# Layer 0 of a four-layer graph network: where the 1/norm broadcast, the rank prefix sums and the rank loads stand in the order of work

## The chip, the cores and the metric

The kernel runs on one NeuronCore of a Trainium2 chip. It is one launch, and all four layers are in it. The metric is the time of an execution on the device in microseconds (us). Three runs of the kernel before took 1393.85, 1397.64 and 1398.86 us; the median is 1397.64 us. The profile is of a further execution, which took 1403.91 us, with a span of 1402.0 us from the first instruction to the last.

## The reference, cut to what matters

N = 2708 nodes, D = 512 features, `adj` is a sparse N x N matrix of float32 values with a nonzero diagonal, denser in its first rows and columns. Only layer 0 is touched by the change:

```python
h = maximum(layernorm(x), 0)                     # (N, D)
head = (adj > 0).astype(float32)
head = head / maximum(sqrt(sum(head * head, axis=-1, keepdims=True)), 1e-12)
inc = adj + head                                 # = adj + mask * 1/norm of the row
x = x + (inc @ h) / sum(inc, axis=-1, keepdims=True)
```

`head * head` summed over a row is the number of nonzeros of the row, so a row needs one number for its head, `rn` = 1/sqrt(count), and one for its degree. Layer 1 (attention, which for these scores comes down to the largest entry of each row of `adj`), layer 2 (two products with `adj`, two dense layers) and layer 3 (a product with the mask of `adj`) follow.

## The kernel before, in words

The rows are cut in 22 tiles of 128 (the last has 20). In layer 0 the loop at L780 to L838 takes one row tile m after the other. Its product `inc @ h` is not done over all 2708 columns: the first six column tiles (DENSE = 6) are taken whole, and of the rest only the columns in which one of the tile's rows has a nonzero. These are found on the chip, per row tile, and are brought in by indirect DMAs on POOL in chunks of 128 columns (CHUNKS, L39: 8 chunks for tile 3, 7 for tiles 4 to 7, 6 for 8 to 14, 5 or 6 for 15 to 20, 2 for 21). Row tiles 0 to 2 (LEAD) are taken over all columns.

For a row tile k >= 3 the steps are these, and they are spread over several passes of the loop:

- Row statistics, `row_norm` and `row_sum` (L523, L543): the slab `ar` of 128 full rows (1354 KB) is loaded, ACT takes the signs (L534), their count (L538), rn (L539) and the row sum (L549). `attended` (L555) takes the largest entry of each row and its place on DVE (L561, L562). Slabs have three buffers.
- `count` (L292): for each group of three row tiles PE adds the signs up over the rows (L302), which gives for each column the number of nonzeros that each row tile has in it.
- `rank_blocks` (L343): DVE makes 0 or 1 of the counts and sums them over each quarter of the columns (L351). PE turns the sums into the offset of each quarter (`ahead`, L355), ACT copies it (L356), DVE scans (L357) and adds the end mark (L358), and SP writes the result, the rank of each column, to DRAM in four pieces (`rank_b`, L361). For the last row tile and for tiles 1 and 2, `rank_rows` (L366) does the same in one row each, from the counts in DRAM (L375, L376, L379), and is put on the list `todo` as a job of its own.
- `load_ranks` (L387): SP reads the ranks of one row tile back, the same row to all 128 partitions (485 KB; two buffers).
- `search` (L400): DVE looks up the place of the 1st, 2nd, 3rd ... nonzero column in the ranks (L407, L409, L413) and writes the indices idx_g and idx_a (L414, L422).
- `gather_adj` (L566): POOL gathers the columns of `adj` (tile `ac`, three buffers, 64 KB each chunk). `gather_rows` (L586): POOL gathers the rows of h into the slots of `h` (16 slots, 256 KB each chunk).
- `incidence` (L624): PE spreads the rn of the 128 rows along the free axis (`rb`, L629, a PSUM tile with one buffer). DVE makes inc = adj + mask * rb for the dense columns (tile `inc`) and for the listed ones (tile `incl`), in two instructions each (L634, L642). The listed `ac` is written to DRAM for the later layers (L657, `lst`).
- Products (L792): first six dense ones, then the listed ones, into one PSUM bank. Every product is a matmul of float32, which the profile shows as two PE instructions.
- `after` (L725): the projection of tile m - 2 (L158, four products) and the transposes of tile m - 1 (L192). Then DVE scales and adds (L805) and normalizes for layer 1 (L176 to L186).

The jobs on `todo` are done by `do_next` (L677): one for each row tile whose statistics are made, and, once all are made, one for each pass of the loop, two in passes 15 and 16. Before a search runs, its ranks are loaded, and after each call the ranks of the next search are. `stats_to` (L688) holds the statistics up to eight row tiles ahead of the products. `gathers_to` (L716) gathers the columns of tile m + 3 and the rows of tile m + 2 at the end of pass m, where the search is done by then. `flush` (L755) issues the stores that were put off.

The order on each engine's queue is set by a scheduler at build time, which keeps the order of the program where costs and due times don't tell otherwise. `tc.issue_after(ins)` puts what is traced in its block behind `ins` on that instruction's engine. [...]

In pass m the incidence of tile m + 1 is traced ahead of the products of tile m (L787, L788).

Of the kernel before, what the change touches and what calls it, by code (L numbers as in the profile page):

```python
# [9 lines left out]
FP = mybir.dt.float32  # L10
# [12 lines left out]
P = 128  # L23
# [13 lines left out]
DENSE = 6  # L37
LEAD = 3
# [4 lines left out]
def kernel(  # L43
# [31 lines left out]
    NT = (N + P - 1) // P  # L75
# [52 lines left out]
    WIDE, LOW = (N - BEHIND) // 4, BEHIND // 2  # L128
# [97 lines left out]
    with tc.tile_pool(name="l0_slab", bufs=2) as slabs, tc.tile_pool(  # L226
        name="l0_h", bufs=1
    ) as hp, tc.tile_pool(name="l0_w", bufs=2) as wp, tc.tile_pool(
        name="l0_acc", bufs=2, space=PSUM
    ) as ps_acc, tc.tile_pool(name="l0_small", bufs=1, space=PSUM) as ps_small, tc.tile_pool(  # L230
        name="l0_list", bufs=3, space=PSUM
    ) as ps_list, tc.tile_pool(name="l0_tr", bufs=1, space=PSUM) as ps_tr, tc.tile_pool(
        name="l0_y", bufs=1, space=PSUM
# [109 lines left out]
        def rank_blocks(ms, last_block):  # L343

            wide = WIDE
            row_end = hp.tile([P, WIDE + 1], HF, name="rk")
            rk, end = row_end[:, :wide], row_end[:, wide : wide + 1]
            sums, offs = (wp.tile([P, 1], FP, name=name) for name in ("sums", "offs"))  # L350
            nc.vector.tensor_scalar(  # L351
                rk, last_block, 1.0, None, op0=ALU.min, op1=ALU.add, accum_out=sums
            )
            ahead = ps_list.tile([P, BLK], FP, name="list")
            nc.tensor.matmul(ahead[:, :1], ahead_of, sums, start=True, stop=True)  # L355
            nc.scalar.copy(offs, ahead[:, :1])  # L356
            nc.vector.tensor_tensor_scan(rk, rk, rk, offs[:, 0:1], ALU.add, ALU.max)  # L357
            nc.vector.tensor_scalar_add(end, row_end[:, wide - 1 : wide], 1.0)  # L358
            for b in range(4):
                w = wide + b // 3  # L360
                nc.sync.dma_start(  # L361
                    out=rank_b[ms[0] // GROUP, : len(ms), b * wide : b * wide + w],
                    in_=row_end[b * QUAD : b * QUAD + len(ms), :w],
                )
# [22 lines left out]
        def load_ranks(m):  # L387
            first = dense_of(m) * P
            num = N - first
            if first:  # L390
                ranks = slabs.tile([P, N + 1 - BEHIND], HF, name="ranks", bufs=2)
                q = m % GROUP
                row = rank_b[m // GROUP, q : q + 1, : num + 1]
            else:
                ranks, row = in_slab(), rank_l
            ranks = ranks[:, : num + 1]
            nc.sync.dma_start(out=ranks, in_=row.to_broadcast([P, num + 1]))
            ranks_of[m] = ranks
# [273 lines left out]
        listable = set()  # L672


        todo = []

        def do_next(num=1):  # L677
            for job in todo[:num]:
                if job.func is search and job.args[0] not in ranks_of:
                    load_ranks(job.args[0])  # L680
                job()
                if job.func is search:
                    listable.add(job.args[0])
            del todo[:num]
            if todo and todo[0].func is search and todo[0].args[0] not in ranks_of:
                load_ranks(todo[0].args[0])

        def stats_to(m):  # L688


            while normed[0] <= order_n.index(m):
                t = order_n[normed[0]]
                do_next()
                load_slab(t)
                if normed[0] + 1 < NT:
                    load_slab(order_n[normed[0] + 1])
                row_norm(t)
                row_sum(t)
                if t == 0 or t % GROUP == GROUP - 1 or t >= NT - 2:
                    last_block = count(masks)  # L700
                    if t not in ZERO:
                        if dense_of(t):
                            rank_blocks(list(masks), last_block)
                        else:
                            flush_counts()
                            todo.append(partial(rank_rows, list(masks)))
                        todo.extend(partial(search, k) for k in masks)
                        do_next(0)
                    masks.clear()
                if t in LATE:  # L710
                    slab.pop(t)
                else:
                    attended(t)
                normed[0] += 1
# [65 lines left out]
        for m in range(NT):  # L780
# [3 lines left out]
            if m + 2 < NT and m + 2 >= LEAD and dense_of(m + 2):  # L784
                blocks[m + 2] = load_block(m + 2, tiles_d)
            flush()
            if LEAD <= m + 1 < NT:  # L787
                incs[m + 1] = incidence(m + 1)  # L788
            acc = ps_acc.tile([P, D], FP, name="acc")
            pairs = incs.pop(m)  # L790
            for i, (a, g) in enumerate(pairs):
                product = nc.tensor.matmul(  # L792
                    acc[:n], a, g, start=(i == 0), stop=(i == len(pairs) - 1)
                )
                first_of_sum = first_of_sum if i else product.ins
            if m + 1 < LEAD:
                stats_to(m + 1)
                incs[m + 1] = incidence(m + 1)
            if m > 1:
                with tc.issue_after(first_of_sum):  # L800
                    after(m - 2, None)
            if m:
                after(m - 1, hns.pop(m - 1))
# [5 lines left out]
            norm(wp, xt, n, hns[m])  # L809
            store(m, xt)  # L810
            if normed[0] == NT:
                do_next(2 if NT - 8 < m < NT - 5 else 1)
            stats_to(min(2 * m + 6, m + 8, NT - 1))
            gathers_to(m + 2)

# [477 lines left out]
    FIRST = 2  # L1293
# [505 lines left out]
```

## Time and profile before

| what | value |
|---|---|
| median of three runs | 1397.64 us |
| profiled execution | 1403.91 us, span 1402.0 us |
| PE busy in the span | 1274.1 us (91%) |
| DVE, ACT, POOL busy in the span | 931.4, 689.0, 655.7 us |
| row tiles 3 to 21 of layer 0 | products from 129.9 to 441.2 us |
| end of layer 0 | last projection from 459.2 to 462.8 us |
| first matmul of layers 1 and 2 | 481.2 us |

Times in the profile are in us from the start of the span, means of one instruction in ns. A line of a view of waits reads: engine, what it wanted to do, what it waited for, the sum, how often, the longest. A line of a timeline reads: start, duration, engine, line of the kernel, operation, tiles written and read, how many instructions, and in brackets the idle time before it and what ended that. A line of a table by windows reads: window, its length, then the busy time of PE, of PE's weight loads, of DVE, ACT and POOL (with the number of instructions), the granted TensorE clock, the mean busy share of the 16 DMA engines, and GB/s.

### The profile page before, as it was taken

To read this page: it belongs to the slowest core of one execution; us is meant where nothing else is said; L and a number is where in the kernel's file an instruction comes from. 1 tells how busy PE (TensorE), PEld (TensorE's weight loads), DVE (VectorE), ACT (ScalarE), POOL (GpSimd) and SP (SyncE) were. 2 spreads that over 40 slices of the span, in tenths; PEclk is the share of its full clock that TensorE was granted. 3 is DMA by queue.
4 is the path that set the end of the run, shared out by engine and by line. 5 is a ranking of instruction groups with operands and counts; after the bars stand their busy time and mean duration, and the time that the engine had idled before them with its cause. 6 is when DMAs were issued, how large, how long until landed. Compare 5 with 4: busy or idle time off the path is not lost. (4 is left out here: it accounts for less than half of the span.)

```text
span 1402.0 us, 15500 instructions
## 1 busy us (share of the span) xinstructions
PE 1274.1 (91%) x4478; PEld 768.7 (55%) x4478; DVE 931.4 (66%) x1760; ACT 689.0 (49%) x1051; POOL 655.7 (47%) x702
## 2 busy tenths in 40 slices
PE   4889989979988489999999999899999999978997
PEld 2334434434433267655656666466666666646886
DVE  4787989886997588623434446365566656658786
ACT  5885737733354466413333335244455544546553
POOL 2255677776555311165444441333334344634762
PEclk9999999999999799999999999999999999979999
DMA  9999899998993975487777777856555666748984
GB/s 345 357 325 316 305 327 356 326 336 266 306 341 107 302 251 196 129 276 252 255 210 240 229 230 221 264 172 193 168 166 170 198 203 187 240 146 287 302 279 161
DMA packets 188461, 348.35 MB, mean 248 GB/s; under 512 B 22174, under 2 KB 98868, under 8 KB 184636
## 3 DMA queue, kind: packets, MB, share of 16 engines
q1 hardware_dynamic: 140768, 200.13, 42.6%
q0 software_dynamic: 46032, 145.05, 32.5%
q10 hardware_dynamic: 1568, 2.10, 0.4%
q8 instruction: 37, 0.61, 0.2%
q14 instruction: 56, 0.46, 0.1%
HBM read 284.59 MB, written 62.61 MB: 248 GB/s over the span
## 5 line engine op out<-in xcount | busy, mean ns | idle before, releaser
L1014 PE MATMUL aggs<-gg,ac 128*128 128x512 f32 (+1 forms) x520 | 232.4, 594 | 4.3 <-DMA gg<-g1d,idx_g 4.3
L962 POOL DMA_INDIRECT gg<-g2d,idx_g x130 | 131.0, 1008 | 218.2 <-PE aggs L1014 169.1
L962 POOL DMA_INDIRECT gg<-g1d,idx_g x130 | 133.3, 1025 | 173.7 <-PE aggs L1014 103.7
L792 PE MATMUL acc<-h,inc 128*128 128x512 f32 (+1 forms) x348 | 168.0, 631 | 10.7 <-DVE inc L642 10.7
L573 POOL DMA_INDIRECT ac<-in_adj_t_dram,idx_a x130 | 131.2, 1009 | 93.9 <-issue 32.6
L1014 PEld LDWEIGHTS aggs<-gg,ac 128*128 128x128 f32 (+1 forms) x520 | 97.6, 189 | 111.1 <-issue 101.2
L592 POOL DMA_INDIRECT h<-h0d,idx_g x111 | 114.2, 1028 | 34.9 <-issue 20.7
L998 ACT ACTIVATE a_hi<-raw 128x384 fp32r<-128x384 f32 x84 | 43.6, 520 | 160.6 <-issue 87.2
L1011 PE MATMUL agg<-ghi,a_hi 128*128 128x512 f32 x252 | 115.5, 458 | 3.9 <-ACT a_hi L998 3.6
L792 PEld LDWEIGHTS acc<-h,inc 128*128 128x128 f32 (+1 forms) x348 | 66.8, 201 | 87.8 <-issue 72.7
L1011 PE MATMUL agg<-glo,a_lo 128*128 128x512 f32 x252 | 101.9, 404 | 3.5 <-ACT glo L207 3.5
L1011 PE MATMUL aggs<-gs,a_s 128*128 128x512 f32 x252 | 100.0, 400 | 0.8 <-DVE gs L204 0.7
L792 PE MATMUL acc<-h,incl 128*128 128x512 f32 (+1 forms) x222 | 100.5, 599 | 0.0
L999 DVE TENSOR_TENSOR a_lo<-raw,a_hi 128x384 fp32r<-128x384 f32 x84 | 47.2, 562 | 76.5 <-ACT a_hi L998 49.6
L908 DVE SCALAR_TENSOR_TENSOR v_lo<-pt,v_hi 128x512 fp32r<-128x512 f32 (+1 forms) x88 | 56.6, 664 | 44.9 <-ACT v_hi L907 44.4
L158 PE MATMUL yacc<-wvo,hT 128*128 128x512 f32 (+1 forms) x176 | 82.4, 611 | 1.0 <-ACT hT L193 1.0
L962 POOL DMA_INDIRECT gg<-hidr,idx_h x62 | 63.6, 1026 | 41.8 <-PE aggs L1202 15.7
L889 DVE SCALAR_TENSOR_TENSOR u<-aggs,u 128x512 f32<-128x512 f32 x42 | 28.8, 687 | 77.5 <-PE aggs L1014 75.9
L792 PEld LDWEIGHTS acc<-h,incl 128*128 128x128 f32 (+1 forms) x222 | 42.1, 192 | 52.0 <-issue 49.1
L907 ACT ACTIVATE v_hi<-pt 128x512 fp32r<-128x512 f32 (+1 forms) x88 | 48.6, 578 | 43.7 <-PE pt L902 41.9
L180 ACT ACTIVATE rstd<-mv,eps 128x1 f32<-128x1 f32 x88 | 24.5, 289 | 83.2 <-DVE mv L178 61.1
L562 DVE FIND_INDEX8 at_top<-tops,ar 128x8 uint32<-128x2708 f32 (+1 forms) x22 | 65.3, 2970 | 0.0
(326 smaller groups left out, 2781.7 us busy)
## 6 DMA issues: line engine op xcount, KB each, us to landing
ar<-in_adj_dram SPq DMA_DIRECT2D x27, 1354.0 KB
raw<-in_adj_t_dram SPq DMA_DIRECT2D x122, 192.0 KB
slot<-x SPq DMA_DIRECT2D x41, 256.0 KB
at<-in_adj_t_dram SPq DMA_DIRECT2D x27, 384.0 KB
ranks<-rank_b SPq DMA_DIRECT2D x20, 485.2 KB
ac<-lst SPq DMA_DIRECT2D x16, 384.0 KB
h<-in_x_dram SPq DMA_DIRECT2D x21, 256.0 KB
h0d<-h POOLq DMA_DIRECT2D x21, 256.0 KB, 5.7
```

Of the source, the lines that this page charges most:

```text
L158: nc.tensor.matmul(acc[:n], hT[:, c, :n], w[:, c, :], start=(c == 0), stop=(c == NCD - 1))
L562: nc.vector.max_index(at_top[:n, m, :], tops[:n, m, :], ar[:n])
L573: nc.gpsimd.indirect_dma_start(out=ac[:, c, :n], out_offset=None, in_=adj_units, element_offset=dense_of(m) * P * N + m * P, in_offset=bas ...
L592: nc.gpsimd.indirect_dma_start(out=g, out_offset=None, in_=h0d[:, :], in_offset=bass.IndirectOffsetOnAxis(ap=idx_g[:, m, c : c + 1], axis=0),)
L792: product = nc.tensor.matmul(acc[:n], a, g, start=(i == 0), stop=(i == len(pairs) - 1))
L907: nc.scalar.activation(hi[d], pt[d], AF.Relu, scale=UP)
L908: nc.vector.scalar_tensor_tensor(lo[d], pt[d], 0.0, hi[d].bitcast(FP), op0=ALU.max, op1=ALU.subtract)
L962: nc.gpsimd.indirect_dma_start(out=gs[c], out_offset=None, in_=gd[:, :], in_offset=bass.IndirectOffsetOnAxis(ap=index[:, m, c : c + 1], ax ...
L998: nc.scalar.activation(hi[d], raw, AF.Copy, scale=UP)
L999: nc.vector.tensor_tensor(lo[d], raw, hi[d].bitcast(FP), ALU.subtract)
L1011: nc.tensor.matmul(acc[:n], a[:k, i, :n], b[:k], start=st, stop=sp)
L1014: nc.tensor.matmul(mixed[:n], a, g, start=(c == 0 and not dense_of(m)), stop=(c == len(chunks) - 1),)
```

## The change

Four edits, all in layer 0. First, `rank_blocks` is cut in two: what is left of it ends with the sums (L351), and a new function `rank_rest` does the offset on PE, the copy on ACT, the scan and the end mark on DVE and the four writes on SP. `rank_rest` goes on `todo` as a job ahead of the group's searches (for the first group, tiles 3 to 5, it is done at once). Its matmul is queued behind the first product of the running row tile. Where it follows the job that is taken, it is taken along with it. Second, the incidence of tile m + 1 is traced inside the loop over the products of tile m, behind the sixth dense product. Third, `do_next` loads the ranks of up to two searches ahead. Fourth, two jobs are done in pass 17 as well.

```diff
             rk, end = row_end[:, :wide], row_end[:, wide : wide + 1]
-            sums, offs = (wp.tile([P, 1], FP, name=name) for name in ("sums", "offs"))
+            sums = wp.tile([P, 1], FP, name="sums")
             nc.vector.tensor_scalar(
                 rk, last_block, 1.0, None, op0=ALU.min, op1=ALU.add, accum_out=sums
             )
+            return partial(rank_rest, ms, row_end, sums)
+
+        def rank_rest(ms, row_end, sums):
+
+            wide = WIDE
+            rk, end = row_end[:, :wide], row_end[:, wide : wide + 1]
+            offs = wp.tile([P, 1], FP, name="offs")
             ahead = ps_list.tile([P, BLK], FP, name="list")
             nc.tensor.matmul(ahead[:, :1], ahead_of, sums, start=True, stop=True)
             nc.scalar.copy(offs, ahead[:, :1])
...
-        todo = []
+        todo, first_of_sum = [], [None]
 
         def do_next(num=1):
+            if num and todo[num:] and todo[num].func is rank_rest:
+                num += 1
             for job in todo[:num]:
                 if job.func is search and job.args[0] not in ranks_of:
                     load_ranks(job.args[0])
-                job()
+                if job.func is rank_rest:
+                    with tc.issue_after(first_of_sum[0]):
+                        job()
+                else:
+                    job()
                 if job.func is search:
                     listable.add(job.args[0])
             del todo[:num]
-            if todo and todo[0].func is search and todo[0].args[0] not in ranks_of:
-                load_ranks(todo[0].args[0])
+            for job in todo[:2]:
+                if job.func is not search:
+                    break
+                if job.args[0] not in ranks_of:
+                    load_ranks(job.args[0])
...
                         if dense_of(t):
-                            rank_blocks(list(masks), last_block)
+                            rest = rank_blocks(list(masks), last_block)
+                            if t == FIRST[-1]:
+                                rest()
+                            else:
+                                todo.append(rest)
...
             flush()
-            if LEAD <= m + 1 < NT:
-                incs[m + 1] = incidence(m + 1)
             acc = ps_acc.tile([P, D], FP, name="acc")
             pairs = incs.pop(m)
             for i, (a, g) in enumerate(pairs):
                 product = nc.tensor.matmul(
                     acc[:n], a, g, start=(i == 0), stop=(i == len(pairs) - 1)
                 )
-                first_of_sum = first_of_sum if i else product.ins
+                first_of_sum[0] = first_of_sum[0] if i else product.ins
+                if i + 1 == min(DENSE, len(pairs)) and LEAD <= m + 1 < NT:
+                    with tc.issue_after(product.ins):
+                        incs[m + 1] = incidence(m + 1)
...
             if m > 1:
-                with tc.issue_after(first_of_sum):
+                with tc.issue_after(first_of_sum[0]):
                     after(m - 2, None)
...
             if normed[0] == NT:
-                do_next(2 if NT - 8 < m < NT - 5 else 1)
+                do_next(2 if NT - 8 < m < NT - 4 else 1)
```

## The prediction

> **What bounds the kernel now.** I read the row of 40 slices first, then a table by stage, the waits of each engine in the stage that the change touches, and last the timelines around the longest waits. By stage:
>
> ```profile
> 130.00:440.00 310.00, 280.51 (x775) 128.17 (x775) 275.97 (x453) 159.34 (x198) 200.59 (x197) 0.96 0.90 310
> 130.00:346.00 216.00, 194.37 (x557) 88.78 (x556) 186.69 (x317) 116.51 (x144) 147.84 (x151) 0.95 0.94 323
> 142.00:312.00 170.00, 152.38 (x451) 69.78 (x449) 153.72 (x253) 97.85 (x118) 125.04 (x126) 0.96 0.95 330
> 440.00:482.00 42.00, 17.73 (x61) 6.71 (x59) 22.36 (x64) 16.41 (x27) 19.14 (x21) 0.74 0.67 213
> 482.00:1402.00 920.00, 876.08 (x3334) 590.58 (x3332) 544.59 (x1032) 413.65 (x698) 381.77 (x376) 0.98 0.69 218
> ```
>
> The stage of the change is 130 to 440 us (tiles 3 to 21). No one thing bounds it: in 310 us PE is busy 280.5, DVE 276.0, and the DMA engines 90%. POOL looks free (200.6), but from 142 to 312 us it issued 126 gathers, one each 1.35 us, with hardly a gap: it is as full there as the others. After 482 us PE is busy 95% of the time and no edit touches it, so what the stage wins or loses arrives at the end as it is, through a change of layer (440 to 482 us) that hangs on the last projection of layer 0. The waits in the stage, of PE, DVE and POOL:
>
> ```profile
> PE rb L629 <- DVE incl L634: 13.1, 3, 7.0
> PE list L355 <- DVE rk L351: 11.0, 3, 8.9
> ...
> DVE ends L407 <- DMA ranks<-rank_b: 25.1, 7, 7.9
> ...
> POOL ac L573 <- DMA lst<-ac: 27.2, 5, 10.6
> ```
>
> These are the waits that the change aims at: the 1/norm broadcast (L629) and the offset matmul (L355) stand in PE's queue ahead of products that could run, and the searches on DVE wait for ranks. PE's timeline shows a second price:
>
> ```profile
> 189.74 0.77 PE L629 MATMUL rb<-ident,rn 128*128 128x128 f32 x2 [5.72 <-DVE incl L634]
> 190.30 7.22 PE L792 MATMUL acc<-h,inc 128*128 128x512 f32 x12
> 208.87 5.32 PE L792 MATMUL acc<-h,inc 128*128 128x512 f32 x12
> 314.36 0.59 PE L355 MATMUL list<-sums,ahead_of 128*128 128x1 f32 x2 [8.85 <-DVE rk L351]
> 314.81 3.76 PE L792 MATMUL acc<-h,inc 128*128 128x512 f32 x4
> 318.36 6.34 PE L792 MATMUL acc<-h,incl 128*128 128x512 f32 x12
> 397.10 0.77 PE L629 MATMUL rb<-ident,rn 128*128 128x128 f32 x2 [6.98 <-DVE incl L634]
> ```
>
> Twelve dense instructions take 5.32 us, but 7.22 us behind the 5.72 us wait.
>
> **What the Trainium skill says.** "TensorE: Matmul & The Clock Gate", Part 1: an idle window of about 3.4 us puts the array back to half clock until it has been busy for such a window. The trace agrees: matmuls behind waits of 5.72, 8.85 and 6.98 us are slow at first, those behind 1.91 us (262.64) are not. "DMA: Bandwidth & Descriptors", Issuing engines are not separate DMA queues: DMAs of all queues share the 16 engines. It agrees: with SP and POOL issuing, the share is 0.94 up to 346 us. The same page, Specifications: about 1 us to the first byte of a DMA from GpSimd; here a gather holds POOL for 1.01 to 1.03 us and the next starts 1.25 us after it. The same page, Anatomy of one DMA: a wait is served by the issuing queue before dispatch. So a load of ranks that waits on SP holds what stands behind it; the trace has 8.6 us between the last rank write (169.0) and the first rank load (177.6).
>
> **The change part by part.** I count against the profiled execution (1403.91 us, span 1402.0). The median is 6.27 us lower, and I take the same difference from it.
>
> *Broadcast behind the dense products.* Same instructions, moved 12 dense ones (5.3 us) later. At 189.74 the dense products would run in the 5.72 us wait, and the listed ones need the `incl` that ended at 190.74 anyway: 5.3 us and the 1.9 us of slow clock, 7 us. At 397.10 six products already stood ahead; the other 2.7 us could go in, but DVE is busy 10.0 of 10 us in each slice from 380 to 430 us and sets the pace: zero. The price is on DVE: it gets rb(m+1) later, and its four instructions (3.7 us) must end before the next tile's dense products. Behind rb stand the listed products (5.3), projection (3.6) and transposes (0.6), 9.5 us: covered, with some 5 us over. If DVE is later than that, the excess is PE's.
>
> *Offset matmul ahead of the dense products, one tile later.* Its sums are then a tile old, so the 11.0 us go, and 3.0 us of slow clock behind the 8.85 (3.76 for 1.8, 6.34 for 5.3). DVE, ACT and SP do the same work later; ACT's copy stood at 0.7 us of DVE's waiting. It costs nothing itself, but the searches move one tile later, some 14 us.
>
> *Ranks two ahead, searches a tile later.* The 25.1 us of DVE waits are four groups of 4.7, 6.1, 1.6, 7.9 and a last one of 4.7. From the end mark (L358) to the first search they took 12.2 to 16.9 us. With a tile between, I take away all but 2 us for the first group. The second load needs the buffer of the search before, so SP can stall there as it did (8.4 us before, on DVE's found), hidden while `xt`, `ar` and `at` behind it are early.
>
> *What is late next: POOL.* In the built order POOL now issues 23 row gathers before tile 6's columns, where it had 16, then tiles 6 and 7 together. Walking DVE's new order with the durations of before, the search of tile 6 ends at about 159 instead of 136. Before:
>
> ```profile
> 130.46 0.95 POOL L592 DMA_INDIRECT h<-h0d,idx_g  x1 [0.30 <-PE rb L629]
> 142.01 0.94 POOL L573 DMA_INDIRECT ac<-in_adj_t_dram,idx_a  x1 [10.61 <-DMA lst<-ac]
> 275.40 0.94 POOL L592 DMA_INDIRECT h<-h0d,idx_g  x1 [0.30 <-DMA ac<-in_adj_t_dram,idx_a]
> ```
>
> The last row gather of tile 12 is the 100th from 142.01 and was issued at 275.4. In the new order it is the 93rd from about 160: at 1.28 (without the 8 us of gaps) to 1.35 us, it comes at 279 to 285, 3 to 9 us later. It lands about 7.4 us after (median of such gathers), and PE wanted it at 295: 12 us to spare before. So PE can be ahead by 3 to 9 us at tile 12, I take 6, whatever stalls have gone. Then the 8.85 us stall and its slow clock fall out at tiles 13 and 14, where POOL is already past: 6 + 12 = 18 us ahead at 346 us.
>
> *DMA engines.* Up to 346 us they were busy 0.94 of 216 us, 203 us, so at full share 13 us can be won. Shares of 1.03 and 1.04 occur in single slices, so it is no sharp wall: between 13 and 18, I take 15.
>
> *The end of the layer.* `rank_rows` and the search of its first tile now fall in the same pass. For tile 1, DVE had 15.1 us between the end mark (L379, 383.8) and the search (398.95) and didn't wait. In the new order there stand 7.9 us of work (0.27, 0.93, 2.96, 0.80, 2.97). Against round trips of 12.2 to 16.9 us that is 4.3 to 9.0 us of new wait, on a DVE that is full: I take 5. For tile 21 the work between is about 13 us: 0 to 4, taken as 0. The projections, last y and the y gathers keep their order: 0.
>
> Sum: 15 - 5 = 10 us. 1402.0 - 10 = 1392 in span, 1397.6 - 10 = 1387.6 as a median; I say 1387.
>
> **The rivals.** *All stalls go* and PE alone paces: 29.5 us of PE idle and some 8 of slow clock are there; POOL's count allows 18 us until 346, and up to 6 more could come of the 9.6 us of stall and slow clock at 397, so 24 us: 1373. For it: DVE was busy 97% of the 70 us from 190 to 260. Against: the DMA share. *The DMA engines are the bound*: the ranks come early, but slabs, lists and gathers come later by as much, and waits on DMA take the place of those removed: within 3 us, 1395 to 1400. For it: 0.94. Against: DMA had slack at 140 (0.74) and 320 us (0.77). *Slower*: the searches of tiles 21 and 1, now in the pass of their rank rows, wait on DVE for the whole trip, up to 9 us each, and 3 us more each for the counts (L375 waited 3.0 before), 24 us in all, behind them `inc`, `xt` and the last `attended` scans. It decides once these waits exceed what was won before 346 us: with 15 won it ends 9 us slower, 1407. That the broadcast isn't moved can't be: in the built order it stands behind the six dense products of each tile from 3 on.
>
> **How the numbers follow.** Forecast (7 to 18 us won) 0.50; all stalls gone 0.12; DMA bound, or gains given back, 0.23; slower 0.15. About 0.5% (7 us) is what a measurement of this kernel can tell from no change. Faster 0.62, same 0.23, slower 0.15. The range runs from 1374 (the PE rival's edge) to 1404 (short of the slower case); the forecast's own is 1380 to 1391.
>
> **What would show it.** L629 and L355 no longer head PE's waits in layer 0; L407 waits below 10 us; POOL's gather for tile 6 starts near 160 and then runs without gaps; tile 12's listed products end about 6 us earlier than 296, tile 15's dense ones start 13 to 18 us earlier than 346; L407 waits 5 us at tile 1. It is wrong if tile 6's columns come after 170 us, if DVE waits more than 15 us for ranks late in the layer, or if the stage after 482 us changes its length.

## The result, and the profile after

The changed kernel takes as long as the kernel before: 1400.75 us against 1399.03 us (medians of 20 runs each), a ratio of 1.0015 with a 95% interval of 1.0000 to 1.0030. Two repeats of the same pair gave 0.9999 (0.9977 to 1.0022) and 1.0005 (0.9987 to 1.0022). The forecast was 1387 us. Of the runs below, some had a kernel before of 1401 us beside them, close to the first measurement (together called setting A), the others one of 1464 to 1477 us (setting B), and a ratio is always to the kernel before that ran beside it.

The profiled execution of after has a span of 1400.7 us (before 1402.0). The stages, with the same columns as in the prediction (stretch, its length, busy time of PE, PEld, DVE, ACT and POOL, granted clock, DMA share, GB/s):

```profile
130.00:346.00 216.00, 202.89 (x577) 92.42 (x576) 194.31 (x325) 118.73 (x149) 151.09 (x142) 0.96 0.95 331
346.00:440.00 94.00, 82.46 (x198) 36.44 (x196) 78.47 (x125) 40.18 (x50) 57.37 (x57) 0.91 0.77 263
...
482.00:1402.00 920.00, 874.64 (x3321) 588.84 (x3319) 541.40 (x1022) 411.61 (x693) 380.28 (x374) 0.98 0.68 216
```

Up to 346 us PE was busy 8.5 us longer than before (202.89 against 194.37) and DVE 7.6 us: the kernel is ahead. The stage after 482 us is the same. So the lead is lost between 346 and 482 us. The waits of PE and of DVE from 120 to 450 us in the changed kernel (total, times, longest):

```profile
PE acc L810 <- DVE inc L649: 14.2, 5, 5.1
PE acc L810 <- DMA h<-h0d,idx_g: 8.2, 3, 4.3
```

```profile
DVE ends L414 <- DMA ar<-rank_l: 7.5, 1, 7.5
DVE ends L414 <- DMA ranks<-rank_b: 6.8, 5, 2.7
```

The two waits that the change aimed at, 24.1 us of PE, are gone, and the 25.1 us of DVE for ranks have become 14.3 us, of which 7.5 are a new one: for the ranks of tile 21 (`rank_l`). PE now waits for `inc` and for row gathers instead. Its timeline shows where (the dense products of tiles 15, 17 and 18, and the first matmul of layers 1 and 2):

```profile
334.28 6.94 PE L810 MATMUL acc<-h,inc 128*128 128x512 f32 x12 [3.39 <-DVE inc L649]
...
369.24 8.22 PE L810 MATMUL acc<-h,inc 128*128 128x512 f32 x12 [5.14 <-DVE inc L649]
...
390.19 7.99 PE L810 MATMUL acc<-h,inc 128*128 128x512 f32 x12 [4.34 <-DVE inc L649]
...
477.65 1.97 PE L923 MATMUL pt<-ident,slot 128*128 128x128 f32 x8 [16.74 <-ACT slot L186]
```

A dense part that doesn't wait takes 5.3 to 5.4 us; behind the waits it takes 1.6 to 2.9 us longer. The starts of the dense products of a tile, in all profiled executions of setting A (us; the rows below tile 20 are the copy of the last projection, POOL's last list store, which is for tile 2, the first matmul of layers 1 and 2, and the time from there to the end of the span):

| | before | before_here | after | after_here | after_here2 | late_back6 |
|---|---|---|---|---|---|---|
| tile 6 | 190.3 | 185.0 | 178.2 | 178.2 | 178.6 | 178.4 |
| tile 12 | 285.8 | 286.4 | 277.3 | 277.3 | 277.7 | 277.3 |
| tile 15 | 346.0 | 345.4 | 334.3 | 334.6 | 333.6 | 332.7 |
| tile 16 | 359.7 | 359.0 | 349.5 | 350.0 | 349.8 | 348.0 |
| tile 17 | 374.1 | 373.4 | 369.2 | 367.9 | 366.5 | 362.4 |
| end of 18's dense | 402.7 | 398.6 | 398.2 | 396.3 | 395.8 | 394.5 |
| tile 20 | 425.3 | 421.1 | 422.1 | 421.7 | 418.8 | 416.3 |
| last projection copied | 462.9 | 458.9 | 461.0 | 461.1 | 458.3 | 450.1 |
| POOL's last list store | 457.8 | 455.2 | 453.6 | 453.0 | 450.7 | 452.3 |
| first matmul of next layers | 481.2 | 478.6 | 477.7 | 478.2 | 474.8 | 473.9 |
| from there to the end | 920.8 | 922.7 | 923.1 | 920.1 | 915.1 | 918.0 |

before_here, after_here and after_here2 are the unchanged kernels once more, late_back6 is an experiment. After is 10.8 to 12.4 us ahead at tile 15, whichever executions are compared. Between the mean of its three and the mean of the two of before, the lead is 11.6 us there, 3.9 at the end of tile 18's dense products, 2.3 at tile 20, 0.7 at the last projection and 3.0 at the first matmul of the next layers. So all but 0.7 us is gone before layer 0 ends. The two executions of before differ by 5 us at tile 6 and agree again by tile 12: the wait at the offset matmul near 262 us was 5.38 us in before_here and 1.91 in before. What follows the first matmul varies by 8 us among kernels that are equal there.

### The profile page after: what moved, and what is told of

It is laid out like the page before. It is cut to its first block, busy times and chain, and to the rows that moved or that the text cites. A ratio compares the mean times of both kernels' runs of the same rounds, so it can differ in the third digit from the quotient of the medians.

```text
span 1400.7 us, 15489 instructions
## 1 busy us (share of the span) xinstructions
PE 1278.7 (91%) x4478; PEld 770.3 (55%) x4478; DVE 932.4 (67%) x1760; ACT 689.2 (49%) x1051; POOL 662.4 (47%) x702
## 4 chain that ended last, share of the span: by engine, by line
PE 63%; DMA 17%; DVE 9%; issue 4%; ACT 3%; POOL 2%; SPq 0%; DVEq 0%; ACTq 0%; POOLq 0%
PE aggs L1035 15%; PE main L948 10%; PE agg L1032 8%; PE acc L810 6%; DMA h<-h0d,idx_g 5%; PE mixed L948 4%; PE aggs L1032 4%; PE agg L1223 3%; PE aggs L1223 3%; PE pt L923 3%; PE yacc L158 2%; PE aggs L1047 2%; DVE found L420 1%; PE pt L1223 1%; DMA wa<-in_L_gnn_Wo_dram 1%
## 5 line engine op out<-in xcount | busy, mean ns | idle before, releaser
L580 POOL DMA_INDIRECT ac<-in_adj_t_dram,idx_a x130 | 139.2, 1071 | 62.2 <-issue 32.6
L810 PE MATMUL acc<-h,incl 128*128 128x512 f32 (+1 forms) x222 | 104.7, 618 | 8.2 <-DMA h<-h0d,idx_g 8.2
L568 DVE MAX8 tops<-ar 128x8 f32<-128x2708 f32 (+1 forms) x22 | 65.4, 2972 | 0.1
```

The source lines that it names most:

```text
L568: nc.vector.max(tops[:n, m, :], ar[:n])
L580: nc.gpsimd.indirect_dma_start(out=ac[:, c, :n], out_offset=None, in_=adj_units, element_offset=dense_of(m) * P * N + m * P, in_offset=bas ...
L810: product = nc.tensor.matmul(acc[:n], a, g, start=(i == 0), stop=(i == len(pairs) - 1))
```

## The experiments

Theory A: the lead is won up to tile 15 and given back at tiles 15 to 18, because the rank row of tile 21 and the search of tile 21 now share a pass. Theory B: DVE is full from 346 us on, so what is taken away at one tile comes up at the next. (From 346 to 404 us DVE was busy 55.3 of 58 us in before, and 45.6 in after, which doesn't fit a full DVE: 11.8 us of the rest are waits for ranks and for ACT.) One kernel has several labels where it ran in more than one setting or pair.

### Late passes as in the kernel before

```diff
-                do_next(2 if NT - 8 < m < NT - 4 else 1)
+                do_next(2 if NT - 9 < m < NT - 5 else 1)
```

This is the changed kernel, with tile 21's rank row and search in two passes again. One kernel under six labels. The first:

> The changed kernel, but the passes with two jobs are those of tiles 14 to 16 (not 15 to 17), so rank_rows of tile 21 and its search fall in different passes again, as in the kernel before. Theory A (won up to tile 15, given back at tiles 15 to 18 by tile 21's rank row and search in one pass): no scan of tile 21's row ahead of tile 15's incidence and no 7.5 us wait of DVE for tile 21's ranks; tile 15's dense products start near 334 us as in the changed kernel, tile 20's by 414 (changed 422, before 425), the first matmul of layers 1 and 2 near 469 (changed 477.7), median 8 to 10 us below the changed kernel. Theory B (DVE is full from 346 us on, so what is taken away at one tile comes up at the next): tile 20's dense products within 2 us of 422, first matmul of layers 1 and 2 at 476 to 479, median within 3 us of the changed kernel.

Setting B: 1.0016 (0.9985 to 1.0048). Four repeats:

> A repeat, on another chip, of the changed kernel with two jobs in the passes of tiles 14 to 16 (changed: 15 to 17), so that rank_rows of tile 21 and its search fall in different passes as in the kernel before; on the first chip layer 0 took some 75 us longer in every kernel, so that its stage can't be set beside the traces of the kernels before and after. Theory A (won up to tile 15, given back at tiles 15 to 18 by tile 21's rank row and search in one pass): no 7.5 us wait of DVE for tile 21's ranks; tile 15's dense products start near 334 us, tile 20's by 414 (changed 422, before 425), first matmul of layers 1 and 2 near 469 (changed 477.7), median 8 to 10 us below the changed kernel, 0.993 to 0.995 of the kernel before. Theory B (DVE is full from 346 us on, so what is taken away at one tile comes up at the next): tile 20's dense products within 2 us of 422, ratio to the kernel before 0.999 to 1.003.

> The same kernel as late_back, tried once more because layer 0 took some 75 us longer in every kernel on the chip of the runs so far, with waits of 5 to 25 us whose releaser the trace doesn't show, which bury a difference of 10 us. Expected on a chip where the kernel before takes about 1399 us. Theory A: tile 15's dense products start near 334 us, tile 20's by 414, first matmul of layers 1 and 2 near 469, ratio to the kernel before 0.993 to 0.996. Theory B (DVE's volume from 346 us on sets the end): tile 20's dense products within 2 us of 422, ratio 0.999 to 1.003.

> The changed kernel with two jobs in the passes of tiles 14 to 16 (changed: 15 to 17), on a chip where the kernel before takes about 1400 us. Theory A (won up to tile 15, given back at tiles 15 to 18 because tile 21's rank row and search share a pass): DVE's 7.5 us wait for tile 21's ranks goes; tile 15's dense products start at 331 to 336 us, tile 20's by 414 (changed 422, before 421 to 425), first matmul of layers 1 and 2 near 469 (changed 478), ratio to the kernel before 0.992 to 0.996. Theory B (from 346 us on DVE's queue holds more than the products leave time for, whatever the pass): tile 20's dense products within 2 us of 422, ratio 0.998 to 1.002. On a chip with 1465 to 1475 us it tells nothing of either.

> The kernel of late_back4, sent alone, for a chip where the kernel before takes about 1400 us. Theory A (given back at tiles 15 to 18 because tile 21's rank row and search share a pass): DVE's 7.5 us wait for tile 21's ranks goes; tile 15's dense products start at 331 to 336 us, tile 20's by 414 (changed 422, before 421 to 425), first matmul of layers 1 and 2 near 469 (changed 478), ratio to the kernel before 0.992 to 0.996. Theory B (from 346 us on DVE's queue holds more than the products leave time for, whatever the pass): tile 20's dense products within 2 us of 422, ratio 0.998 to 1.002. If it is slower than before by 1% here too, both fall.

All in setting B: 1.0101 (1.0049 to 1.0153), 1.0108 (1.0065 to 1.0152), 1.0120 (1.0071 to 1.0169), 1.0061 (1.0034 to 1.0089). With the first pair, the same kernel was at 1.0016 to 1.0120 in setting B. So it is slower there by 0.2 to 1.2%, which neither theory has, and a single pair in setting B is uncertain by about 1%. Setting A, beside the changed kernel:

> The kernel of late_back5, beside the changed kernel. Where the kernel before takes about 1400 us, theory A: tile 20's dense products by 414 us, first matmul of layers 1 and 2 near 469, ratio 0.992 to 0.996; theory B: 0.998 to 1.002. Where it takes 1465 to 1476 us: 1.006 to 1.012 as measured; theory A then wants it 0.005 or more below after_here2, theory B within 0.003 of it.

Setting A: 0.9988 (0.9963 to 1.0014), the changed kernel beside it 1.0005. The ratio is theory B's, but tile 20's products start at 416.3 us, which is neither A's 414 nor B's 422. The trace of late_back6 says more than the ratio. PE at tiles 17 and 18 and at the next layers:

```profile
362.43 5.32 PE L810 MATMUL acc<-h,inc 128*128 128x512 f32 x12
...
386.24 8.27 PE L810 MATMUL acc<-h,inc 128*128 128x512 f32 x12 [10.11 <-DVE inc L649]
...
473.89 1.11 PE L923 MATMUL pt<-ident,slot 128*128 128x128 f32 x4 [23.84 <-ACT slot L186]
```

DVE's wait for tile 21's ranks is gone, and so is PE's wait at tile 17 (theory A is right in that). The scan of tile 21's row still stands ahead of tile 15's `inc`, and the wait there stays (3.48 us). And the wait at tile 18 is 10.11 us, where the changed kernel had 4.34, 5.44 and 7.14. In the 26 us from tile 16's `xt` (360.43) to tile 18's `inc` (386.2) DVE stood still for 2.02 us; the rest is work that now comes together: the scan of tiles 1 and 2 (4.17), tile 21's search (2.97), an `attended` (5.9) and the weight split (5.2). That is theory B, at this tile. Of 4 to 7 us won over the changed kernel at tile 17, 1 to 4 are left at the end of tile 18's dense products.

The second thing is at the end. The last projection is copied at 450.13 us, 8 to 11 us earlier than in the changed kernel and 8.8 and 12.7 us earlier than in the two executions of before. So up to there theory A's lead is back, in this one execution. The first matmul comes only 1 to 4 us earlier than in the changed kernel (4.7 and 7.3 earlier than before); PE waits 23.84 us for it (changed 16.5 to 17.2). POOL, SP and ACT in late_back6:

```profile
452.28 0.57 POOL L590 DMA_DIRECT2D lst<-ac  x1 [1.23 <-DMA ac<-in_adj_t_dram,idx_a]
...
463.07 0.99 POOL L1088 DMA_INDIRECT slot<-y,idx  x1 [10.23 <-DMA slot<-x]
```

```profile
454.57 1.76 SPq L1086 DMA_DIRECT2D slot<-x  x4
...
457.16 0.31 SPq L758 DMA_DIRECT2D y<-yo  x1
```

```profile
450.13 0.57 ACT L756 COPY yo<-yacc 20x512 f32<-20x512 f32 x1 [4.41 <-PE yacc L158]
454.76 1.67 ACT L197 ACTIVATE wb<-wr 128x512 fp32r<-128x512 f32 x3 [4.05 <-DMA lst<-ac]
```

POOL's last list store is issued at 452.28 us. ACT's `wb`, whose releaser the trace names as `lst<-ac`, starts 2.5 us later; SP's first load for the next layers (`slot<-x`) and DVE's `idx_h` (454.78) start within 0.2 us of it. They are the first users of buffers that layer 0 gives back. (That this is why they wait is argued: the trace names `lst<-ac` for ACT and SP, and nothing for DVE.) The last rows of y were ready at 450.7 us, but their write stands in SP's queue behind `slot<-x` and goes out at 457.16; the first gather of y starts at 463.07. So in this execution the change of layer has a second limit behind the last projection: POOL's queue, with SP's order after it.

Which limit applies can be read from the 20 profiled executions of both settings. In 13 of them, both of before and this one among them, the first `slot<-x` goes out 2.3 to 2.5 us after the issue of POOL's last list store. In the other 7, all three of after among them, it goes out 2.8 to 4.0 us after that store, and 0.5 us after the start of the copy of the last-but-one projection, which is where this copy ends. All 7 have rank row and search of tile 21 in one pass. In all 8 kernels of that kind the copy comes 2.3 to 3.6 us after POOL's last store, in the other 12 between 7.3 us before it and 0.2 after it. So the pairing makes the projections late against POOL's queue. In the changed kernel it isn't shown that POOL's queue sets the end.

### The late pairing alone

```diff
-                do_next(2 if NT - 8 < m < NT - 5 else 1)
+                do_next(2 if NT - 7 < m < NT - 4 else 1)
```

The kernel before, with rank row and search of tile 21, and of tile 1, in one pass.

> The kernel before with only its late passes changed: two jobs in the passes of tiles 16 and 17 (before: 15 and 16), so that the rank rows of tiles 21 and 1 and the searches behind them fall in one pass each, as in the changed kernel. Theory A (this pairing costs the give-back): DVE waits 5 to 10 us for tile 21's ranks and PE waits for inc at tiles 17 and 18; start of tile 15's dense products as before (346 us), first matmul of layers 1 and 2 at 485 to 490 us (before 481.2), ratio to the kernel before 1.003 to 1.008. Theory B: the wait is there but within DVE's slack or replaced by another: ratio 0.998 to 1.002.

> The same kernel as late_only, once more for the same reason. Theory A: DVE waits 5 to 10 us for tile 21's ranks and PE waits for inc behind it; tile 15's dense products as before at 346 us, first matmul of layers 1 and 2 at 485 to 490 us (before 481.2), ratio to the kernel before 1.003 to 1.008. Theory B: ratio 0.998 to 1.002.

> The kernel before with two jobs in the passes of tiles 16 and 17 (before: 15 and 16), so that the rank rows of tiles 21 and 1 share a pass with the search behind them, on the same chip. Theory A: DVE waits 5 to 10 us for tile 21's ranks; tile 15's dense products at 345 to 346 us, first matmul of layers 1 and 2 at 484 to 490 us (before 478.6 to 481.2), ratio 1.003 to 1.008. Theory B: DVE and PE wait elsewhere by that much less: ratio 0.998 to 1.002.

All in setting B: 1.0059 (1.0023 to 1.0096), 1.0049 (1.0024 to 1.0074), 1.0057 (1.0033 to 1.0081). The pairing costs 0.5 to 0.6%, some 8 us, as theory A has it. (The text of after_here2 below counts four such runs; three were made.) The cause that A names isn't there: after 300 us DVE's waits for ranks add up to 0, 3.3 and 8.4 us in the three traces, waits of searches without a named releaser to 9.1, 4.5 and 0.2, and none is for tile 21's. Tile 21's load goes out 1.3 us after the write of its row. So the loss is shown, in setting B, and its cause is open.

### The broadcast alone, and all but the broadcast

```diff
-            if LEAD <= m + 1 < NT:
-                incs[m + 1] = incidence(m + 1)
...
+                if i + 1 == min(DENSE, len(pairs)) and LEAD <= m + 1 < NT:
+                    with tc.issue_after(product.ins):
+                        incs[m + 1] = incidence(m + 1)
```

> The kernel before with only the incidence of the next tile put behind the sixth dense product. Theory A: the 5.7 us at 189.7 go with their slow clock, the 8.9 us offset stall at 314 stays; tile 12's dense products start 5 to 9 us earlier than 285.8, tile 15's 5 to 9 us earlier than 346; late rank rows stand as in the kernel before, so it is kept: median 3 to 7 us below the kernel before. Theory B (DVE limits late): at tile 15 as in A, but the median within 2 us of the kernel before.

> A repeat, on another chip, of the kernel before with only the incidence of the next tile put behind the sixth dense product. Theory A: the 5.7 us at 189.7 go with their slow clock, the 8.9 us offset stall at 314 stays; tile 12's dense products start 5 to 9 us earlier than 285.8, tile 15's 5 to 9 us earlier than 346, and it is kept: ratio to the kernel before 0.995 to 0.998. Theory B (DVE limits late): at tile 15 as in A, but ratio 0.999 to 1.002.

Setting B: 1.0006 (0.9977 to 1.0036) and 1.0010 (0.9987 to 1.0033). Theory B's number: moved alone, the broadcast wins nothing that can be measured in this setting. The opposite, the changed kernel with this one edit taken back:

> The changed kernel with the incidence of the next tile back ahead of the products; the ranks are split and loaded two ahead, with the late passes of the changed kernel. Theory A: the 8.9 us offset stall is gone but waits for inc at the broadcast come back (10 to 13 us in all); tile 15's dense products start at 337 to 342 us (changed 334.3), the late give-back of some 14 us is the same: median 2 to 6 us above the changed kernel. Theory B (DVE limits late): median within 2 us of the changed kernel.

Setting B: 1.0049 (1.0021 to 1.0077). The changed kernel wasn't measured in setting B, so the 2 to 6 us of theory A can't be tested; what can be said is that this kernel is slower than before there. It has the late pairing too, which alone cost as much (1.0049 to 1.0059), so nothing is shown of the rest of the rank part.

### The rest of group 6 to 8 at once

```diff
-                            if t == FIRST[-1]:
+                            if t in (FIRST[-1], 8):
                                 rest()
```

Added to the late passes as before. It keeps the searches of tiles 6 to 8 where the kernel before had them.

> As late_as_before, and the rest of the ranks of group 6 to 8 is done at once, so that the searches of tiles 6 to 8 come one tile earlier and POOL doesn't stand for 16 us at 143 to 159 us. Theory A with POOL as the limit up to tile 12 (the changed kernel's PE waits 4.3 us for a row gather at tile 12, 290 us): the waits for h at tiles 6 and 12 go, at the price of a list wait at tile 6 of some 5 us as before; tile 13's dense products start at 295 to 298 us (changed 300.4, before 301.9), median 2 to 5 us below late_as_before. Theory B (DVE or the DMA engines limit): the waits for h go but PE waits for inc instead, median within 2 us of late_as_before. Against both: the early searches push tile 4's and 5's work on DVE back and it is slower by 1 to 4 us.

> A repeat, on another chip, of late_back with the rest of the ranks of group 6 to 8 done at once, so that POOL doesn't stand for 16 us at 143 to 159 us. If POOL is the limit up to tile 12 (the changed kernel's PE waits 4.3 us for a row gather at 290 us): the waits for h at tiles 6 and 12 go, tile 13's dense products start at 295 to 298 us (changed 300.4, before 301.9), ratio 0.002 to 0.004 below that of late_back. If DVE or the DMA engines limit: PE waits for inc instead of h, ratio within 0.0015 of late_back's. Against both: the early searches push tile 4's and 5's work on DVE back, ratio 0.001 to 0.003 above it.

Setting B: 1.0021 (0.9987 to 1.0055) and 1.0000 (0.9974 to 1.0026). Late_back, beside the second, was at 1.0101: here the edit is worth 1%, in the first pair (1.0016 and 1.0021) nothing. The traces agree on what it does: POOL's standstill ahead of tile 6's gathers is 9.3 us in late_back_rest8 (until 146.4), and 18.0 in late_back3 without it (until 168.9).

Whether POOL's late start costs time stays open: the two pairs don't agree, the 1% is no more than the kernel without the edit varies by (1.0016 and 1.0101), and it wasn't measured in setting A.

### The weight split at the end of the layer

```diff
-            if m == NT // 2 + 5:
+            if m == NT - 1:
                 w1 = split_w(
```

> The changed kernel with the split of the weights w1 (5.2 us of DVE) moved from tile 16's pass to the last tile's, behind which PE waits 16.7 us anyway. Theory A: only PE's stall at tile 18 (4.3 to 5.4 us and 2.1 to 2.7 of slow clock) goes: tile 20's dense products start at 414 to 417 us, first matmul of layers 1 and 2 at 470 to 473, ratio to the kernel before 0.994 to 0.997. Theory B (DVE's queue is the bound from 346 us on): the same, since 5 us of DVE's work are gone, so the two differ at late_back alone. Against both (the end of the layer hangs on the gather of y and its norm, not on the products): tile 20's products come earlier, the first matmul of layers 1 and 2 stays at 477 to 479, ratio 0.999 to 1.002.

Setting B: 1.0038 (1.0011 to 1.0065). In this setting there is no changed kernel to set it beside, so whether DVE's volume or the end of the layer decides isn't told by it.

### The two kernels unchanged

> The changed kernel unchanged, on the chip of the experiments, where layer 0 took 65 to 75 us longer in every kernel so far. If the waits without a shown releaser come with the chip and not with an edit, it has them too, between 95 and 450 us, and its ratio to the kernel before is within 0.005 of the 1.0015 of the first measurement. Theory A: late_back, measured at 1.010 and 1.011 on such a chip, is then at least 0.005 slower than this one for a reason that lies in where these waits fall, not in the late passes. Theory B: this one is as slow as late_back (1.008 to 1.012).

> The kernel before unchanged, on the same chip: a null test and a trace to set the others beside. Ratio 0.998 to 1.002. If the 65 to 75 us come with the chip, it shows waits of 5 to 25 us on DVE, PE and ACT without a shown releaser between 95 and 450 us, the same 9 us offset wait at L355 among the others, and the stage after layer 0 of the same length as in the first trace of before (920 us from the first matmul of layers 1 and 2 to the end).

> The changed kernel beside late_back6, on whichever chip. Where the kernel before takes about 1400 us: ratio 0.998 to 1.003 as before. Where it takes 1465 to 1476 us: it has not been measured there. If the pairing of rank row and search costs there what late_only shows (1.005 to 1.006, four times), it is at 1.004 to 1.010; if late_back's 1.006 to 1.012 are what the early part of the change costs there, it is at 1.010 or above; if the change is as neutral there as on the other chip, 0.999 to 1.003, and late_back's loss is then its own.

Setting A: after_here 0.9999, before_here 0.9991 (0.9967 to 1.0015; this is the kernel before beside itself, so it shows the noise), after_here2 1.0005. None of the waits of PE, DVE and ACT without a releaser that setting B shows is in their traces. The first of these runs were on a chip (number 9) that had shown setting B in two earlier groups of runs, so the setting doesn't come with the chip alone. Since the changed kernel itself never met setting B, the question of what it is worth there stays open.

## Why the prediction was wrong

**Broadcast, 7 us at tile 6.** Right in mechanism: the wait at 189.7 us is gone, tile 6 starts 6 to 12 us earlier. Moved alone, it shows no gain in time in setting B (rb_only, rb_alone); in setting A that wasn't measured.

**Offset matmul, 14 us.** Right in mechanism: L362 is in no list of waits. Ahead at tile 15 the two edits together are 10.8 to 12.4 us, where I took 15 and the range was 13 to 18.

**POOL late at tile 6.** Right, with its number, but not priced at tile 6 itself, where PE waits 3.71 us for a row gather and the twelve listed instructions behind it take 8.19. I had the gathers for tile 6 start at about 160 us:

```profile
159.10 0.95 POOL L599 DMA_INDIRECT h<-h0d,idx_g  x1 [16.34 <-issue]
160.35 0.94 POOL L580 DMA_INDIRECT ac<-in_adj_t_dram,idx_a  x1 [0.30 <-issue]
```

At tile 12 PE waits for a row gather as it was to, but the gain there is smaller than the 6 us I took. The changed kernel at tile 12:

```profile
290.48 3.78 PE L810 MATMUL acc<-h,incl 128*128 128x512 f32 x4 [4.26 <-DMA h<-h0d,idx_g]
```

The wait is followed by slow projections (4.78 us against 3.60), and tile 13 starts 1.2 to 4.4 us earlier than before.

**Ranks, 25.1 us of DVE.** Most of the early waits are gone: 6.8 us remain in five waits (9.0 and 3.5 us in the two repeats), where 2 were to be left.

**The end of the layer: this is the step that failed.** It said that tile 21 costs "0 to 4, taken as 0", tile 1 5 us, and that "the projections, last y and the y gathers keep their order: 0". Measured: tile 21 7.5, 7.0 and 6.7 us in the three executions, tile 1 0.8, 1.9 and 0. The 13 us of work between end mark and search were right: DVE was busy 13.7. The way of the ranks to DRAM and back was mis-sized: 24.1 us from the end mark (339.5) to the search, where I had 12.2 to 16.9. What I left out is where the load of tile 21's ranks stands in SP's queue. Changed kernel, SP:

```profile
339.99 0.26 SPq L387 DMA_DIRECT2D rank_l<-ar  x1
350.96 0.35 SPq L764 DMA_DIRECT2D xt<-in_x_dram  x1
...
353.08 0.95 SPq L404 DMA_DIRECT2D ar<-rank_l  x1
```

and DVE:

```profile
363.62 0.15 DVE L414 CAST ends<-ar 128x1 f32<-128x1 f16 x1 [7.50 <-DMA ar<-rank_l]
...
366.65 0.94 DVE L641 SCALAR_TENSOR_TENSOR inc<-at,rb 128x768 f32<-128x768 f32 x1
```

and in the kernel before, SP:

```profile
360.75 0.25 SPq L380 DMA_DIRECT2D rank_l<-ar  x1
...
363.27 0.32 SPq L397 DMA_DIRECT2D ar<-rank_l  x1
```

The row is written at 339.99 us, and its load is issued 13.1 us later (before: 2.5 us), because a load of `xt` that stands ahead of it waits 10.7 us, until 350.96, for a store of `xt` (`x<-xt`). The load itself then takes 10.5 us until DVE can go on. This is the place that I had quoted from the Trainium skill for the early ranks ("DMA: Bandwidth & Descriptors", Anatomy of one DMA: the issuing queue serves the wait) and hadn't applied to the late ones. This trace agrees, by the 10.7 us. The order of DVE does the rest: behind the wait stand the rest of an `attended` and then `inc` of tile 17, for which PE waits 5.14 us and then runs slow for 2.9.

Two more waits of PE, 3.39 us at tile 15 and 4.34 at tile 18, come of DVE's order, where the prediction had taken the price on DVE as "covered, with some 5 us over" and added only "If DVE is later than that, the excess is PE's". At tile 15 the scan of tile 21's row stands ahead of `inc` (and DVE had stood still 4.71 us for ACT before that), at tile 18 the weight split stands between the two halves of `inc`. DVE in the changed kernel:

```profile
325.94 5.78 DVE L383 TENSOR_TENSOR_SCAN ar<-ar 1x2708 f16<-1x2708 f16 x1
...
331.69 0.93 DVE L641 SCALAR_TENSOR_TENSOR inc<-at,rb 128x768 f32<-128x768 f32 x1
```

**The sum.** For the first execution of each kernel: lead at the start of tile 15 11.7 us (I had 15). Lost is the slow clock at tile 15, 1.5, at tile 17 5.14 + 2.90, and at tile 18 4.34 + 2.67, together 16.6. Given back is what the kernel before loses at tile 18, a 6.98 us stall and 2.3 us of slow clock behind it (six dense instructions in 5.07 us instead of 2.74):

```profile
397.65 5.07 PE L792 MATMUL acc<-h,inc 128*128 128x512 f32 x6
```

That leaves 4.4 us, and measured at the end of tile 18's dense products are 4.5. So the account closes up to there; 10 were to be left. From there to the last projection 2.6 us more go. One part of it is seen at tile 20: PE waits 1.90 us for ACT's `hn` (L192), and the dense products behind it take 7.11 us.

**"What the stage wins or loses arrives at the end as it is."** This is wrong as well, though in the changed kernel next to nothing was left to arrive. In late_back6 a lead of 8.8 and 12.7 us over before at the last projection became 4.7 and 7.3 at the first matmul, since POOL's last store came no earlier than in the changed kernel. The changed kernel, POOL, ACT and SP:

```profile
453.64 0.57 POOL L590 DMA_DIRECT2D lst<-ac  x1 [0.87 <-DMA ac<-in_adj_t_dram,idx_a]
456.10 0.59 ACT L756 COPY yo<-yacc 128x512 f32<-128x512 f32 x1 [4.14 <-PE yacc L158]
456.65 0.34 SPq L1086 DMA_DIRECT2D slot<-x  x1
```

The kernel before, POOL and SP:

```profile
457.78 0.57 POOL L583 DMA_DIRECT2D lst<-ac  x1 [1.12 <-DMA ac<-in_adj_t_dram,idx_a]
460.14 0.34 SPq L1065 DMA_DIRECT2D slot<-x  x1
```

The first load of the next layers follows POOL's store in before (by 2.4 us) and the end of the projection's copy in after. Why POOL's last store is hardly earlier can be read from its long gaps. Before, its queue stood still for 10.6 us ahead of tile 6 (see the prediction), 10.59 until 359.37 and 9.86 ahead of tile 1 (until 420.25). In after the first is 16.34 us, the second is gone, and the one ahead of tile 1 stayed (10.21, until 415.42): 31.1 us of long gaps became 26.6. With PE 11 us ahead, POOL was 10 us late (the 60th gather from the last started at 349 us, before at 339). So I had followed POOL's queue up to tile 12, and not to the end of the layer, where it becomes the limit once the projections are early.

**The rivals.** The second, "DMA bound, or gains given back" (1395 to 1400), is nearest, but for another reason than its DMA share: from 346 to 404 us, where most of the lead goes, the share was 0.88, and 0.94 before. The slower one named the right mechanism for tile 21 at a third of its price (8.3 us of DVE waits for tiles 21 and 1, where it had 24). What is left at the first matmul, 3 us between the means of three executions of after and two of before, is less than the 8 us by which the rest of the execution varies; the medians don't show it.

**Open.** In setting A: what stretches POOL's last gathers, so that it is busy only 21.5 of the 54 us from 404 to 458, and where late_back6's lead of 4.7 to 7.3 us at the first matmul goes, since its ratio is 0.9988. In setting B: what the change is worth, why the late pairing costs 0.5% without a wait for tile 21, and why late_back is slower than before. That the pairing costs the lead (theory A) holds up to the last projection and not for the whole time; that DVE's queue takes back most of a wait that is removed at one tile is shown at tile 18 of late_back6, and that POOL's last store caps what is left is shown there too, by one execution each.

## What to carry to other kernels

A lead counts only if the last thing that the next stage waits for is ahead too: follow each engine's queue to the end of the stage, POOL's gathers and stores among them, before a gain in the middle is carried to the end. When a step is moved by one pass, walk the queues of all its parts at its last use as carefully as at its first; the write and the load of tile 21's ranks were the same two DMAs as before, with four others between them in the queue where there had been one. And when an engine is nearly full (DVE was busy 53.2 of the 58 us from 346 to 404 in late_back6), taking away a wait on it moves the work up to the next thing that is late, so price what stands behind it before the wait is counted as won.

## What the runs showed of the hardware

Setting B was not expected. Up to 100 us the timelines are alike (PE busy 70.6 us in rb_alone, 70.4 before); the first matmul of layers 1 and 2 comes at 519 to 543 us instead of 474 to 481, and the rest takes 938 to 950 us instead of 915 to 923. Between 100 and 500 us there are waits, up to 22 us long on DVE and up to 10 on PE, for which the trace names no releaser, and single instructions come in one by one. Late_back3, DVE and then PE:

```profile
217.90 0.95 DVE L641 SCALAR_TENSOR_TENSOR inc<-at,rb 128x768 f32<-128x768 f32 x1 [17.82 <-remote]
```

```profile
213.69 0.34 PE L302 MATMUL list<-sgn,counts 128*32 128x384 bf16 x1 [1.78 <-issue]
```

The count matmuls, which elsewhere run eighteen in 1.29 us, come 2.1 to 3.5 us apart, and DVE stands still until 217.90. The cause isn't known. Differences below 1% between kernels don't carry over from one setting to the other: the same kernel was at 0.9988 in A and at 1.0016 to 1.0120 in B.

How long PE must stand before its clock drops is now known at more points. The Trainium skill ("TensorE: Matmul & The Clock Gate", Part 1) gives a window of about 3.4 us. In the six executions of setting A, from 125 to 440 us, each of the 28 waits of 2.46 us or more was followed by a granted clock of 0.50 to 0.74 over the next 3.5 us. Behind waits of 1.91, 2.05 and 2.19 us it was 1.00, and behind one of 1.90 us (ahead of tile 20 in after) 0.66. So in these traces the drop sets in at about 2 us of waiting, less than the page says. The prediction found the trace of before to agree with 3.4 us; a wait in that trace doesn't: behind 2.51 us (at 149.70) four dense instructions took 3.68 us instead of 1.8. The price doesn't grow evenly with the wait: twelve dense instructions took 5.42 us behind a wait of 2.19 us, 6.94 behind 3.39, 8.22 behind 5.14, 7.45 behind 5.44 and 8.27 behind 10.11. The scan on DVE takes the same per element at one and at three partitions: 5.78 us for 1 x 2708 and 4.17 for 3 x 1940, both 2.1 ns.
